# Output projection of a gated attention block: 16 parts of plain products replaced by one level of Strassen's scheme

## The chip, the cores and the metric

The kernel runs on one core of one Trainium2 chip. The metric is device time in microseconds (us), the median of several executions; the profile is of one execution. A core has five engines, each with one queue of instructions that it works through in order: PE (matrix products, results into the eight PSUM banks), DVE (vector work), ACT (activation functions and copies), POOL (GpSimd) and SP (here only a queue that issues transfers). POOL and ACT issue transfers too. Sixteen DMA engines carry all transfers.

## The reference, cut to what matters

```python
x  = L0_attn_x                                 # (2, 1024, 1024) f32
xn = _layernorm(x)
s  = attention(xn, wq, wk, wv) @ wo            # 32 heads of 32, 8 key heads, causal
g  = silu(ffn(xn, 4-bit weights, zeros, scales))   # 1024 -> 2 x 2752 -> 1024
return x + s * g
```

The change is in the last product of the attention, `out @ wo`: for each of the two batches a 1024 x 1024 matrix `wo` against 1024 tokens of 1024 channels, all in full float32. Its result waits in memory until the feed-forward block multiplies it in at the end.

## The kernel before

**Stages.** In this order: layer norm of batch 0; then for each batch the projections to queries, keys and values (`project`), the attention (`attend`), and the output projection (`project_out`); then the feed-forward block for both batches (`ffn_in_order`), which begins with the products `acc` of L1198. The weights of the feed-forward block come as 4-bit numbers. A generator, `unpack`, turns them into floats unit by unit beside the attention stages: its turns are called from the other stages as `next(side)`.

**The output projection.** `Output.oT` holds the attention's result, 128 partitions by 8 blocks (`NS`) of channels by 1024 tokens. Eight weight tiles `ws` (one for each 128 output channels, each with 8 blocks of 128 input channels) are loaded during the last two key heads. The work is cut into 16 `parts`: 256 tokens by two output blocks. A part is 16 products of 128x128 weights with 256 tokens (L880), eight into each half of one PSUM bank; then `leave` copies the bank to SBUF (L892, by DVE and ACT in turn) and stores it to `sT` (L893, from POOL's or ACT's queue). One float32 product is two matmul instructions in the trace, each with its own weight load.

**Inside the last head.** `first` makes two of the parts while the last key head is attended. It is a generator, and each `next(others)` in `attend` gives out one product of 256 tokens, to fill the time in which PE would wait for ACT's exponentials. The instructions of `attend` are in an order written by hand (`tc.manual_schedule`).

**Beside the other parts.** In `project_out` the order on each engine comes from a planner that lists instructions by program order and by its own estimate of when their inputs come; the queues then run in that order whatever comes late. Batch 0: at the end of each of the first eight parts one tile of batch 1's layer norm (`norm`, L326 to L342) is done: a load on SP's queue, statistics and scaling on DVE, eight transposes on PE, copies on ACT. From part seven on, `side` has `turns` = 3 turns twice in each part. Batch 1: no norm, and `side` has its turns from the first part on; the feed-forward block's inputs `x` and its first weights `w` are loaded at the same time from SP's queue (L946, L937).

**A unit of `unpack`** is four turns: SP loads `qw` and `zt` (L242, L244, two buffers each), DVE makes `nib` (L258, L260, L263), ACT writes `nf` (L267, two instructions of 128x1024), and POOL's queue stores `nf` (L249, 1 MB; two of 512 KB where it goes to `ng`). Batch 0's `project_out` does 8 units, batch 1's does 14. `nf` has the buffers that its pool is opened with: three here, two in the `project` of batch 1. What is left of `side` comes right after `project_out`. The feed-forward block lies in a conditional, so all its instructions stand behind all of `side` on every queue.

## Time and profile before

| | |
|---|---|
| median of 3 runs | 2293.79 us (2292.4 to 2294.47) |
| profiled execution, its own time | 2293.33 us |
| its span in the trace | 2291.6 us |
| granted TensorE clock, mean | 0.993 |
| output projection alone on PE, batch 0 (with 8 norm tiles) | 561.8 to 668 us |
| output projection alone on PE, batch 1 | 1191 to 1290 us |

Times within the trace are counted from the start of the span. A matmul's duration in a row covers its whole way through the array, and successive ones overlap, so the rate at which PE works is read from a stretch: instructions by time. An engine's idle time is put down to what ended it. A row of the timeline or of the chain gives start, length, engine, line and operation; brackets hold the idle time before it and its releaser. A row of windows gives each engine's busy time in a stretch, the granted clock, and the mean busy share of the DMA engines.

### The profile page before, as it was taken

How to read it: one execution, taken by the hardware profiler on the slowest of the kernel's cores; microseconds unless marked ns; L12 is line 12 of the kernel's file. 1: busy time of each engine (PE TensorE's matmuls, PEld its weight loads, DVE VectorE, ACT ScalarE, POOL GpSimd, SP SyncE). 2: the span in 40 equal slices, each digit the busy share in tenths (PEclk: the TensorE clock that was granted, in tenths of full speed). 3: DMA queues.
4: the chain of work that ended last, by engine and by line, in shares of the span. 5: the costliest groups of instructions: out<-in, count | busy, mean ns of one | idle time of the engine just before them, and what ended most of it. 6: DMA issues, size and time to landing. Idle time of an engine off the chain costs nothing.

```text
span 2291.6 us, 30825 instructions
## 1 busy us (share of the span) xinstructions
PE 2239.3 (98%) x11313; PEld 1537.5 (67%) x11313; DVE 1420.2 (62%) x2268; ACT 1132.3 (49%) x1819; POOL 792.4 (35%) x569
## 2 busy tenths in 40 slices
PE   7989999999999999999999999999999999999998
PEld 4455555555874465555558888888877888888875
DVE  5544677773324736777722367667877777777775
ACT  2102544553223325445533455555887555556875
POOL 1303677774035427776741100000234100001362
PEclk9999999999999999999999999999999999999999
DMA  5727323122468971231319623231846655323475
GB/s 180 220 91 244 80 47 93 38 75 76 129 210 280 301 215 47 52 88 38 80 54 344 181 56 83 55 83 55 303 138 219 176 137 139 96 71 105 137 231 154
DMA packets 262183, 309.50 MB, mean 135 GB/s; under 512 B 19147, under 2 KB 197707, under 8 KB 261880
## 3 DMA queue, kind: packets, MB, share of 16 engines
q1 hardware_dynamic: 245172, 260.62, 38.4%
q0 software_dynamic: 10752, 38.02, 5.2%
q10 hardware_dynamic: 6100, 8.82, 1.2%
q8 instruction: 91, 1.49, 0.3%
q14 instruction: 68, 0.56, 0.1%
HBM read 214.58 MB, written 97.03 MB: 136 GB/s over the span
## 4 chain that ended last, share of the span: by engine, by line
PE 82%; issue 7%; POOL 6%; DVE 2%; ACT 2%; DMA 1%; SPq 0%; ACTq 0%; POOLq 0%; DVEq 0%
PE acc L1198 27%; PE acc L1079 12%; PE ps_wo L880 10%; PE st L661 7%; PE s L554 7%; PE o L708 5%; PE ps_qk L384 5%; PE l L726 3%; PE st L676 2%; PE ps_v L407 1%; POOL rot L391 1%; PE s L548 1%; POOL rot L392 1%; POOL p L821 1%; ACT p L686 1%
## 5 line engine op out<-in xcount | busy, mean ns | idle before, releaser
L1198 PE MATMUL acc<-x,w 128*128 128x512 f32 x2752 | 640.1, 393 | 1.2 <-ACT gate L1169 0.9
L1198 PEld LDWEIGHTS acc<-x,w 128*128 128x128 f32 x2752 | 512.3, 188 | 120.5 <-DVE h L1171 7.2
L564 DVE TENSOR_REDUCE mx<-s 128x1 f32<-128x512 f32 (+3 forms) x672 | 384.8, 608 | 190.3 <-PE s L554 91.7
L968 DVE TENSOR_SCALAR acc<-acc,r_gu 128x1024 f32<-128x1024 f32 x301 | 389.1, 1293 | 166.5 <-PE acc L1198 164.9
L686 ACT ACTIVATE p<-st 128x512 f32<-128x512 f32 (+3 forms) x768 | 314.7, 497 | 316.8 <-PE st L676 314.6
L966 ACT ACTIVATE acc<-acc,r_gu 128x1024 f32<-128x1024 f32 x301 | 327.4, 1088 | 231.5 <-PE acc L1198 226.7
L1182 POOL TENSOR_TENSOR h_lo<-h,h_hi 128x512 fp32r<-128x512 f32 x78 | 100.3, 1287 | 805.2 <-DVE h L1160 300.6
L821 POOL TENSOR_TENSOR p<-p 128x2048 f32<-128x2048 f32 (+3 forms) x122 | 360.0, 2955 | 9.0 <-PE o L708 4.6
L968 DVE TENSOR_SCALAR acc<-acc,r_d 128x512 f32<-128x512 f32 x320 | 241.7, 759 | 62.0 <-PE acc L1079 59.3
L966 ACT ACTIVATE acc<-acc,r_d 128x512 f32<-128x512 f32 x320 | 210.8, 663 | 61.8 <-PE acc L1079 55.0
L384 PE MATMUL ps_qk<-xnT,w_qk 128*128 128x512 f32 x512 | 236.0, 602 | 2.5 <-DVE rot L390 2.5
L880 PE MATMUL ps_wo<-oT,w_o 128*128 128x256 f32 x1024 | 232.1, 382 | 0.0
L1079 PE MATMUL acc<-h_lo,w 128*128 128x512 f32 (+1 forms) x576 | 228.9, 397 | 3.0 <-POOL h_lo L1182 2.6
L1079 PE MATMUL acc<-h_hi,w 128*128 128x512 f32 (+1 forms) x576 | 229.5, 398 | 0.7 <-ACT h_hi L1181 0.7
L880 PEld LDWEIGHTS ps_wo<-oT,w_o 128*128 128x128 f32 x1024 | 191.1, 190 | 40.9 <-issue 16.7
L708 PE MATMUL o<-p,v 128*32 128x512 f32 (+3 forms) x1536 | 162.9, 496 | 0.9 <-POOL p L689 0.9
L384 PEld LDWEIGHTS ps_qk<-xnT,w_qk 128*128 128x128 f32 x512 | 94.6, 192 | 99.8 <-issue 93.4
L689 POOL TENSOR_SCALAR_AFFINE_SELECT p<-p 128x512 f32<-128x512 f32 x128 | 80.5, 636 | 163.5 <-ACT p L686 123.0
L391 POOL TENSOR_TENSOR rot<-rot,cs 128x512 f32<-128x512 f32 x40 | 51.3, 1283 | 239.6 <-DVE rot L390 230.2
L554 PE MATMUL s<-kst,room 128*128 128x512 f32 (+3 forms) x384 | 130.4, 379 | 0.0
L1079 PEld LDWEIGHTS acc<-h_lo,w 128*128 128x128 f32 (+1 forms) x576 | 108.4, 188 | 31.0 <-POOL h_lo L1182 5.4
L1079 PEld LDWEIGHTS acc<-h_hi,w 128*128 128x128 f32 (+1 forms) x576 | 108.3, 188 | 30.6 <-issue 2.9
(163 smaller groups left out, 2405.7 us busy)
## 6 DMA issues: line engine op xcount, KB each, us to landing
w<-ng SPq DMA_DIRECT2D x86, 512.0 KB, 5.2
w<-nd SPq DMA_DIRECT2D x63, 512.0 KB, 4.0
ng<-nf POOLq DMA_DIRECT2D x42, 512.0 KB, 6.9
room<-qs SPq DMA_DIRECT2D x160, 128.0 KB, 4.0
x<-xs SPq DMA_DIRECT2D x32, 512.0 KB, 10.2
qst<-qs SPq DMA_DIRECT2D x96, 128.0 KB, 3.8
xt<-in_L_attn_x SPq DMA_DIRECT2D x16, 512.0 KB, 6.2
w_qk<-in_L_attn_wq SPq DMA_DIRECT2D x16, 512.0 KB, 5.0
```

Of the source, the lines that this page charges most:

```text
L384: nc.tensor.matmul(ps, w[:, s, :], xnT[:, s, tok], start=(s == 0), stop=(s == NS - 1))
L554: nc.tensor.matmul(s[:, c * w : (c + 1) * w], q[j][:, qt * P : (qt + 1) * P], k[:, k0:k1], start=n == 1, stop=c == n - 1 and (n > 1 or not ...
L564: nc.vector.tensor_reduce(mx[:, at, js[0] : js[0] + n, k0 // TB], s[:, : w * n].rearrange("p (j t) -> p j t", j=n), AX.X, ALU.max)
L661: nc.tensor.matmul(s[:, q0:], kst[g][:, kt * P : (kt + 1) * P], stack[g][j][:, qlo + q0 : qlo + TB], start=True, stop=False,)
L686: nc.scalar.activation(p[:, j, q0:], st[j][:, q0:], AF.Exp, scale=1.0 / math.sqrt(HD))
L708: nc.tensor.matmul(o[HD * j : HD * (j + 1), q0:], v[:, kt, HD * g : HD * (g + 1)], p[:, j, q0:], start=(kt == 0), stop=last,)
L821: what(*args)
L880: self.last = nc.tensor.matmul(ps[:, c * self.BLK : (c + 1) * self.BLK], self.ws[c0 + c][:, g, :], self.oT[:, g, t0 : t0 + self.BLK], star ...
L966: nc.scalar.mul(a, a, r)
L968: nc.vector.tensor_scalar(a, a, r, None, ALU.mult)
L1079: nc.tensor.matmul(acc[c], w[:k, c * P : (c + 1) * P], ht[:k, :], start=(f == 0 and t == 0), stop=(t == 1), skip_group_check=(f > 0),)
L1198: nc.tensor.matmul(a[:, n, :], w[i][:, g * P : (g + 1) * P], xs[t][:, g, n * TB : (n + 1) * TB], start=(g == 0 and t == 0), stop=(t == 1), ...
```

## The change

The projection of each pair `i` of output blocks (four pairs) becomes one level of Strassen's scheme in Winograd's form. The halves are: output block `c` of the pair, input half `k` (four blocks of 128 channels, `H` = 4), token half `n` (512 tokens). `A[n, k]` are the quarters of `oT`, `weights(i, k, c)` those of the weights. Seven products take the place of eight; each is four matmuls of 128x128 with 512 tokens.

- Sums of the tokens are made once for a batch, by DVE, in 128x2048 pieces: `s1` in a new tile, and three in the places of `A[1, 0]`, `A[0, 0]` and `A[0, 1]` once these have been used.
- Sums of the weights are made for each pair (`quarters`): two by DVE (one into `t_2`), two by POOL, each 128x512.
- Products one and two of every pair come first. Those of pairs 0 and 1 are `first`, inside the last head, with two `yield`s for each product of 512 tokens; DVE copies both. Those of pairs 2 and 3 open `rest`; ACT copies them.
- Then five products for each pair, in two banks `a` and `b`. Each bank is read between its two products: `b` by DVE (`u2`), `a` by ACT (`p5`, to which POOL adds `p1`). Product `fourth` goes into `b` a third time, after the next pair's first product. Four results leave for each pair; of the 16 stores of a batch, 14 are issued by POOL and 2 by ACT, where it was 8 and 8.
- `rest` yields 24 times in a batch, once after each product. `project_out` gives `side` its 3 turns at each (in batch 0 from the eighth on), and the norm's tiles come one after each of the first eight.
- The pool `wo_out` has two buffers for a name instead of four, one for `p_5`, `s_1` and `t_2`. The `unpack` pool of these stages has two buffers instead of three: two for `nf`.

```diff
--- before.py
+++ after.py
@@ -799,7 +799,7 @@
                     output.load(0, NREP + 1)
                 if qb == 0 and kt == 0 and g == NKV - 1:
                     output.load(NREP + 1, NC)
-                    others = output.first(head.ps)
+                    others = output.first(head.ps, kp)
                 if qb == 0 and kt == 0 and 0 < g < NKV - 3:
                     kst.append(key_stack(g + 3))
                 if kt == 0:
@@ -858,12 +858,20 @@
     class Output:
-        BLK = 256
+        H = NS // 2
+        PAIRS = NC // 2
         def __init__(self, b, oT, pool):
             self.b, self.oT, self.pool = b, oT, pool
             self.ws = []
-            self.parts = [(t0, c) for t0 in range(0, T, self.BLK) for c in range(0, NC, 2)]
+            H = self.H
+            self.A = {
+                (n, k): oT[:, k * H : (k + 1) * H, n * TB : (n + 1) * TB] for n in range(2) for k in range(2)
+            }
+            self.p1, self.banks = {}, {}
         def load(self, c0, c1):
             for c in range(c0, c1):
@@ -872,41 +880,122 @@
                 self.ws.append(w)
                 nc.sync.dma_start(w, wo[:, c * P : (c + 1) * P].rearrange("(g p) n -> p g n", p=P))
-        def products(self, part, ps):
-            t0, c0 = part
-            for c in range(2):
-                for g in range(NS):
-                    self.last = nc.tensor.matmul(
-                        ps[:, c * self.BLK : (c + 1) * self.BLK],
-                        self.ws[c0 + c][:, g, :],
-                        self.oT[:, g, t0 : t0 + self.BLK],
-                        start=(g == 0),
-                        stop=(g == NS - 1),
-                    )
-                    yield g
-        def leave(self, part, ps, r):
-            t0, c0 = part
-            copy, queue = ((nc.vector.tensor_copy, nc.gpsimd), (nc.scalar.copy, nc.scalar))[c0 // 2 % 2]
-            copy(r, ps)
-            queue.dma_start(
-                sT_dram[self.b][:, c0 : c0 + 2, t0 : t0 + self.BLK], r.rearrange("p (c t) -> p c t", c=2)
-            )
-        def first(self, pools):
-            r = self.pool.tile([P, 2 * TB], F32, name="wo_r", tag=f"room_{NREP}")
+        def weights(self, i, k, c):
+            return self.ws[2 * i + c][:, k * self.H : (k + 1) * self.H]
+        def product(self, ps, w, x, first):
+            for s in range(self.H):
+                self.last = nc.tensor.matmul(
+                    ps, w[:, s, :], x[:, s, :], start=first and s == 0, stop=s == self.H - 1, skip_group_check=not first
+                )
+                yield
+        def leave(self, i, c, n, y, queue):
+            queue.dma_start(sT_dram[self.b][:, 2 * i + c, n * TB : (n + 1) * TB], y)
+        def first(self, pools, kp):
+            keep = self.pool.tile([P, 2, TB], F32, name="p_1", tag=f"room_{NREP}")
+            r = kp.tile([P, 2, TB], F32, name="wo_r", tag="kst_1")
             for i in range(2):
-                ps = pools[i].tile([P, TB], F32, name="ps_wo", tag=f"s_{i}")
-                part = self.parts.pop(0)
-                yield from self.products(part, ps)
-                self.leave(part, ps, r[:, i * TB : (i + 1) * TB])
+                ps = self.banks[i] = pools[i].tile([P, TB], F32, name="ps_wo", tag=f"s_{i}")
+                for _ in self.product(ps, self.weights(i, 0, 0), self.A[0, 0], True):
+                    yield
+                    yield
+                self.p1[i] = keep[:, i]
+                nc.vector.tensor_copy(self.p1[i], ps)
+            for i in range(2):
+                ps = self.banks.pop(i)
+                for _ in self.product(ps, self.weights(i, 1, 0), self.A[0, 1], False):
+                    yield
+                    yield
+                nc.vector.tensor_copy(r[:, i], ps)
+                self.leave(i, 0, 0, r[:, i], nc.gpsimd)
+        def rest(self, pool, psp):
+            A, weights = self.A, self.weights
+            def bank():
+                return psp.tile([P, TB], F32, name="ps_wo")
+            def product(*args):
+                for _ in self.product(*args):
+                    pass
+            def tile(name, **kw):
+                return pool.tile([P, TB], F32, name=name, **kw)
+            s1 = pool.tile([P, self.H, TB], F32, name="s_1", bufs=1)
+            nc.vector.tensor_tensor(s1, A[1, 0], A[1, 1], ALU.add)
+            nc.vector.tensor_tensor(A[1, 0], A[0, 0], A[1, 0], ALU.subtract)
+            more = range(2, self.PAIRS)
+            for i in more:
+                self.banks[i] = bank()
+                product(self.banks[i], weights(i, 0, 0), A[0, 0], True)
+                self.p1[i] = tile("p_1")
+                nc.scalar.copy(self.p1[i], self.banks[i])
+                yield
+            nc.vector.tensor_tensor(A[0, 0], s1, A[0, 0], ALU.subtract)
+            t2 = {}
+            def quarters(i):
+                t2[i] = pool.tile([P, self.H, P], F32, name="t_2", bufs=1)
+                nc.vector.tensor_tensor(weights(i, 0, 0), weights(i, 0, 1), weights(i, 0, 0), ALU.subtract)
+                nc.vector.tensor_tensor(t2[i], weights(i, 1, 1), weights(i, 0, 0), ALU.subtract)
+                nc.gpsimd.tensor_tensor(weights(i, 0, 1), weights(i, 1, 1), weights(i, 0, 1), ALU.subtract)
+                nc.gpsimd.tensor_tensor(weights(i, 1, 0), weights(i, 1, 0), t2[i], ALU.subtract)
+            quarters(0)
+            for i in more:
+                product(self.banks[i], weights(i, 1, 0), A[0, 1], False)
+                r = tile("u_2")
+                nc.scalar.copy(r, self.banks.pop(i))
+                self.leave(i, 0, 0, r, nc.scalar)
+                yield
+            nc.vector.tensor_tensor(A[0, 1], A[0, 1], A[0, 0], ALU.subtract)
+            def fourth(i, b):
+                product(b, weights(i, 1, 0), A[1, 1], False)
+                nc.vector.tensor_tensor(self.p1[i], b, self.p1[i], ALU.add)
+                self.leave(i, 0, 1, self.p1[i], nc.gpsimd)
+            ahead = None
+            for i in range(self.PAIRS):
+                b = bank()
+                product(b, t2[i], A[0, 0], True)
+                u2 = tile("u_2")
+                nc.vector.tensor_tensor(u2, b, self.p1[i], ALU.add)
+                yield
+                if ahead:
+                    fourth(*ahead)
+                    yield
+                a = bank()
+                product(a, weights(i, 0, 0), s1, True)
+                p5 = tile("p_5", bufs=1)
+                nc.scalar.copy(p5, a)
+                nc.gpsimd.tensor_tensor(p5, p5, self.p1[i], ALU.add)
+                if i + 1 < self.PAIRS:
+                    quarters(i + 1)
+                yield
+                product(b, weights(i, 0, 1), A[1, 0], False)
+                nc.vector.tensor_tensor(p5, b, p5, ALU.add)
+                self.leave(i, 1, 1, p5, nc.gpsimd)
+                yield
+                product(a, weights(i, 1, 1), A[0, 1], False)
+                nc.vector.tensor_tensor(u2, a, u2, ALU.add)
+                self.leave(i, 1, 0, u2, nc.gpsimd)
+                yield
+                ahead = i, b
+            fourth(*ahead)
+            yield
     def project_out(output, side, turns, xnT, xp):
         with ExitStack() as st:
-            res = st.enter_context(tc.tile_pool(name="wo_out", bufs=4, reuse_waits="tile"))
+            res = st.enter_context(tc.tile_pool(name="wo_out", bufs=2, reuse_waits="tile"))
             psp = st.enter_context(tc.tile_pool(name="wo_ps", bufs=6, space=PSUM, reuse_waits="tile"))
             following = iter(())
             w_k = None
@@ -916,20 +1005,17 @@
                 following = norm(output.b + 1, xnT, ln, ln_ps, 3)
                 w_k = load_kv(xp, wk)
             normed = None
-            for i, part in enumerate(output.parts):
-                ps = psp.tile([P, TB], F32, name="ps_wo")
-                for g in output.products(part, ps):
-                    if g == 0 and (xnT is None or i >= NT - 1):
-                        with ExitStack() as order:
-                            for last in normed or ():
-                                order.enter_context(tc.issue_after(last.ins))
-                            for _ in range(turns):
-                                next(side, None)
+            for i, _ in enumerate(output.rest(res, psp)):
+                if xnT is None or i >= NT - 1:
+                    with ExitStack() as order:
+                        for last in normed or ():
+                            order.enter_context(tc.issue_after(last.ins))
+                        for _ in range(turns):
+                            next(side, None)
                 with tc.issue_after(output.last.ins):
                     normed = next(following, normed)
-                output.leave(part, ps, res.tile([P, TB], F32, name="wo_r"))
             return w_k
     def load_gu(ring, f, u):
@@ -1480,7 +1566,7 @@
             xnT = xp = None
         else:
             x_open, xnT, xp = open_x()
-        with tc.tile_pool(name="unpack", bufs=3, side="right", reuse_waits="tile") as up:
+        with tc.tile_pool(name="unpack", bufs=2, side="right", reuse_waits="tile") as up:
             side = unpack(up, range(8) if b == 0 else range(20, NF), b == B - 1)
             w_k = project_out(output, side, 3, xnT, xp)
             for _ in side:
```

## The prediction

> **What bounds the kernel now.** I read the page first (busy shares, chain, costliest groups), then the chain in order of time, the busy time by stretches, and in the two projection stages each engine's timeline and waits.
>
> ```profile
> span 2291.6 us, 30825 instructions
> ...
> PE 2239.3 (98%) x11313; PEld 1537.5 (67%) x11313; DVE 1420.2 (62%) x2268; ACT 1132.3 (49%) x1819; POOL 792.4 (35%) x569
> ...
> L880 PE MATMUL ps_wo<-oT,w_o 128*128 128x256 f32 x1024 | 232.1, 382 | 0.0
> ```
>
> PE is the bound, and the changed line L880 is 232 us of it, 116 a batch, with no idle time before it. The chain shows the rates:
>
> ```profile
> 626.50 41.44 PE ps_wo L880 x192
> 667.94 56.65 PE ps_qk L384 x132
> ...
> 1191.03 99.06 PE ps_wo L880 x458
> ```
>
> An instruction of 256 columns takes 41.44/192 = 0.2158 us, one of 512 columns 56.65/132 = 0.4292 us (L384, same type and weights). So wider matmuls alone win nothing; only fewer products do. The stretches (columns: PE, PEld, DVE, ACT, POOL busy, clock, DMA share, GB/s) show what else is full:
>
> ```profile
> 561.80:668.00 106.20, 106.20 (x527) 93.94 (x524) 34.33 (x83) 31.32 (x49) 20.07 (x26) 1.00 0.67 208
> 1191.00:1290.00 99.00, 99.00 (x463) 87.17 (x460) 23.83 (x67) 30.84 (x35) 18.89 (x23) 1.00 0.93 309
> ```
>
> PE has no gap in either, at a granted clock of 1.00. DVE, ACT and POOL are a third busy or less. But in batch 1 the DMA engines are 93% busy, and the queues that carry the unpacking wait for them (ACT's timeline, then waits, batch 1):
>
> ```profile
> 1249.46 2.00 ACT L267 ACTIVATE nf<-nib 128x1024 fp32r<-128x1024 uint8 x2 [2.32 <-DMA nd<-nf]
> 1253.14 2.00 ACT L267 ACTIVATE nf<-nib 128x1024 fp32r<-128x1024 uint8 x2 [1.68 <-DMA nd<-nf]
> 1257.53 2.00 ACT L267 ACTIVATE nf<-nib 128x1024 fp32r<-128x1024 uint8 x2 [2.38 <-DMA nd<-nf]
> 1259.44 0.56 ACT L892 COPY wo_r<-ps_wo 128x512 f32<-128x512 f32 x1
> ...
> 1277.35 2.00 ACT L267 ACTIVATE nf<-nib 88x1024 fp32r<-88x1024 uint8 x2 [4.97 <-DMA nd<-nf]
> 1279.25 0.56 ACT L892 COPY wo_r<-ps_wo 128x512 f32<-128x512 f32 x1
> ```
> ```profile
> DVE nib L263 <- DMA zt<-zb_d: 17.1, 6, 5.0
> ACT nf L267 <- DMA nd<-nf: 16.8, 7, 5.0
> ```
>
> The copies of finished banks stand in these queues. The tenth part of the stage ended on PE at about 1193 + 10 x 6.9 = 1262; ACT copied it at 1279.25, 17 us late. That cost nothing before: six banks of 6.9 us each are 41 us of room.
>
> **The change part by part.**
>
> *Products.* Per batch, 256 matmuls of 256 columns become 112 of 512; in instructions, 512 x 0.2158 = 110.5 us become 224 x 0.4292 = 96.1 us. `first` keeps its share (32 of 256, then 16 of 112: 13.8 us both), so `rest` falls from 448 x 0.2158 = 96.7 us to 192 x 0.4292 = 82.4 us: 14.3 us a batch, 28.6 in all. A product of `rest` is 3.43 us.
>
> *`first`, inside the last head.* Same work in pieces of 0.86 us at every other turn instead of 0.43 at each. PE was busy 40.8 of 42 us there (520 to 562). Between +1 and -1 us: I take 0. The DVE copies (0.69 us, L892) come when DVE is idle (9.13 us before the last `lt`), and the bank has the other pair's product (3.4 us) before it is written again.
>
> *Token sums.* Four DVE operations of 128x2048. The 128x512 sum of L753 takes 0.68 us undisturbed; four times the elements about 2.3. The last `oT` comes at 1193.6 (batch 1), so `s1` ends at 1196, `A[1,0]` at 1198, `A[0,0]` after products one (1200) at 1202.5; two `quarters` (0.68 each) follow to 1204. PE wants `t_2` at 1193 + 4 x 3.43 = 1207. Hidden, by 3 us. In batch 0, DVE also has norm tiles: 2.4 us each (two statistics 0.65, L329, and L337 0.83, small ones), and PE wants one every 3.43 + 0.88 = 4.3 us instead of every 7.8. Divide, three sums, quarters and five tiles are 2.1 + 6.9 + 1.4 + 12 = 22 us; by the fifth product PE has given 19 to 20. PE waits 2 us (0 if the first loads come before the divide; 5 if sums and late `xt` loads line up).
>
> *Weight sums and `p5`.* Per batch 8 DVE operations (5.4 us), and on POOL 8 plus 4 for `p5` at 1.28 us (L753 on POOL), 15.4 us; the bank sums are 16 reads of 0.7 us, half of them where copies were. DVE goes to about 34 + 9.2 + 5.4 + 5.6 = 54 of 92 us in batch 0, 44 of 85 in batch 1, POOL to 35: room. That two engines' sums collide has a row:
>
> ```profile
> 1161.82 4.57 POOL L821 TENSOR_TENSOR p<-p 128x2048 f32<-128x2048 f32 x1 [2.31 <-PE o L708]
> ...
> 1162.78 4.15 DVE L753 TENSOR_TENSOR oT<-oc,rt 128x512 f32<-128x512 f32 x1
> ```
>
> The DVE sum, 0.68 us elsewhere, lasted until POOL's ended. New POOL operations are 1.28 us, so a collision costs at most that: at most 15.4 us of DVE time a batch, hidden by DVE's idle third. I take 0; the bound is 3 us, the four sums ahead of PE's first need. [...]
>
> *Banks.* This is what the change adds to the path. `a` may be written again only after ACT's `p5`, with one product between (3.43 us of room; before, 41). `p5` stands in ACT's queue among the `nf` that wait for DMA; `u2` and the other sum in DVE's queue among the `nib`; POOL's share of `p5` among the stores. What is late by more than 3.43 us stops PE. Also `p_5` has one buffer: its next copy waits for the store of the last, four products later (13.7 us against 0.7 + 0.75 + 8.7 for sum, issue and landing in batch 1): hidden while POOL isn't 3 us late.
>
> *`nf` with two buffers.* A buffer's cycle in batch 1 is 2.0 (ACT) + 0.3 + 0.86 (POOL's issue) + 8.8 us to landing = 12.0; by three, 4.0 us a unit (the rows above: 3.7 and 4.4). By two, with the landing unchanged, 6.0; with the shortest landing of L249, 3.5 us, 3.3, so nothing lost. The DMA engines were 0.9 to 1.0 busy, so much of the 8.8 is queueing behind the third buffer and falls with it: I take 4.4, nearer the low end.
>
> *Batch 0.* PE alone would end at 668 - 14.3 = 653.7. Unpacking now begins after the seventh norm tile at about 595 (619 before) and takes 8 x 4.6 us (before 34 us) plus waits, to 632 to 635. The `p5` at products 11 and 16 (609 and 626) lie inside; the late ACT copy of 644.17 shows 4 us of lag with three buffers. One stop of 3 us: with DVE's 2, PE loses 5. Gain 14.3 - 5 = 9 (3 to 14).
>
> *Batch 1.* The unpacking is held by 8 MB of `x` and by `w` until 1230 (`qw`, 15.4 us wait), then 13 units, four of 88 rows and a small one. They took 48 us, 12 x 4.0; 12 x 4.4 put the last `nf` at 1284 to 1286 instead of 1279. PE alone would end at 1275.7. But `p5` of the last pair stands near the last `nf`; two products (6.9 us) follow it: 1286 + 0.6 + 6.9 is beyond the old end, 1290, by some 3 us if it stands behind all of them, and before it, 1285, if two units remain. I take a gain of 0.5 (bounds -20 with 6.0 us a unit: 12 x 2 us later; +12 if the lag never reaches PE, since the feed-forward block's ACT work still stands behind the last `nf` at 1279).
>
> *Queues.* SP keeps its loads in number and order. POOL issues 14 instead of 8 stores a batch (0.74 us each): inside its idle 80%.
>
> Sum: 9 + 0.5 = 9.5 us off the profiled execution's 2293.33 (span 2291.6 and 1.7 around it): 2283.8; its median stands 0.46 higher: 2284.
>
> **The rivals.**
>
> *Both stages pay in full.* For it: PE had no gap, engines are two thirds idle, and the planner may set `p5` ahead of `nf`. Against: the 17 us lag. Gain 13 + 11 = 24: 2270.
>
> *Batch 1 gives back what batch 0 brings.* Lag and unpacking hold each other up: ACT waits for PE's `a` while `nf` waits behind it. Some 5 us a unit: last `nf` at 1291, PE's end at 1299, 9 - 9 = 0: 2294.
>
> *Slower: two `nf` buffers hold the stage.* With the landing at 8.8 us a unit takes 6.0; batch 1's last `nf` is at 1303, PE's end at 1310 (-20); batch 0's 8 units end at 643, with PE's stops 10 us (+4). Together -16: 2310. It decides from 5.3 us a unit on: last `nf` at 1294, PE's end at 1302 (-12), batch 0 at +7, so -5, just over 0.2%. Against it: DMA share near 1.0 means that the landing is queueing.
>
> *The saving isn't one*, because 512-column matmuls are slower than two of 256: excluded by 0.4292 against 2 x 0.2158.
>
> **How the numbers follow.** Forecast 0.40 (2278 to 2289), both in full 0.23 (2266 to 2277), given back 0.16 (2289 to 2299), slower 0.21 (2299 to 2312). 0.2%, 4.6 us, is about what a measurement can tell here from no change. Faster 0.63, same 0.16, slower 0.21. The range leaves out the slow half of the last case and the best of the second: 2267 to 2303.
>
> **What would show it.** Right: L880's place holds 2 x 224 instructions of 512 columns at 0.43 us; PE gaps before second and third products into a bank, ended by ACT `p_5` or DVE sums, behind `nf` and `nib` waiting for DMA; batch 1's first `acc` within 5 us of 1290 less batch 0's gain. Wrong: no gaps there (2270), or units at 5.3 us and more (over 2298), or PE waiting in batch 0 for norm transposes by more than 5 us.

## The result, and the profile after

The changed kernel takes 2302.9 us (median of 5 runs, 2300.53 to 2305.48); the kernel before, in the same comparison, 2293.79 (2292.4 to 2296.23). The ratio is 1.0037 with a 95% interval of 1.0026 to 1.0048: slower by 9 us or 0.4%. The forecast was 2284, faster by 0.4%.

Three lines of the page of the changed kernel. L889 is now the projection's matmul, L1284 the feed-forward block's.

```profile
span 2300.8 us, 29810 instructions
...
PE 2216.2 (96%) x10737; PEld 1427.9 (62%) x10737; DVE 1483.4 (64%) x2316; ACT 1132.8 (49%) x1819; POOL 837.2 (36%) x605
...
L889 PE MATMUL ps_wo<-oT,w_o 128*128 128x512 f32 x320 | 153.5, 619 | 20.8 <-ACT p L978 14.4
```

PE does 23 us less (2239.3 before) in a span that is 9.2 us longer. The saving was made, and something else grew by more. The last line says where: before L889 PE is idle for 20.8 us, mostly released by ACT's copy of `p5` (L978). Before the change that column read 0.0.

The two projection stages, as stretches (columns as before: length, then PE, PEld, DVE, ACT and POOL busy, clock, DMA share, GB/s):

```profile
562.80:663.00 100.20, 92.49 (x264) 43.45 (x261) 57.60 (x102) 31.88 (x49) 36.51 (x38) 1.00 0.65 207
1188.60:1299.00 110.40, 90.74 (x198) 38.56 (x196) 50.77 (x87) 31.53 (x36) 39.31 (x38) 0.94 0.85 284
```

Batch 0's stage went from 106.2 to 100.2 us. Batch 1's went from 99.0 to 110.4: its PE work is shorter, but there is a hole of 20 us in it, and the mean granted clock is 0.94 where it was 1.00. The whole difference, cut at the same events in both traces (start of the second-last single mask of batch 0's last head, last sum matmul `l` of L726 in each batch, first `ps_qk` of L384, first `acc` of the feed-forward block, end):

| stretch | before, us | after, us | difference |
|---|---|---|---|
| up to the mask in batch 0's last head | 539.86 | 539.44 | -0.4 |
| from it to the last `l` | 21.60 | 22.98 | +1.4 |
| projection, batch 0 | 106.32 | 100.59 | -5.7 |
| projections and attention of batch 1, up to the same mask | 501.23 | 502.19 | +1.0 |
| from it to the last `l` | 21.60 | 22.99 | +1.4 |
| projection, batch 1 | 99.12 | 110.87 | +11.8 |
| feed-forward block | 1001.87 | 1001.74 | -0.1 |
| span | 2291.6 | 2300.8 | +9.2 |

Two things need an explanation: the projection of batch 1, and 1.4 us in each last head. First the projection, on PE's timeline of the changed kernel (start, length, what, idle time before and its releaser):

```profile
1209.07 3.60 PE L889 MATMUL ps_wo<-s,w_o 128*128 128x512 f32 x8
...
1254.75 5.40 PE L889 MATMUL ps_wo<-oT,w_o 128*128 128x512 f32 x8 [4.32 <-ACT p L978]
...
1268.47 7.13 PE L889 MATMUL ps_wo<-oT,w_o 128*128 128x512 f32 x16 [1.45 <-DVE p L984]
1282.38 5.43 PE L889 MATMUL ps_wo<-oT,w_o 128*128 128x512 f32 x8 [6.79 <-ACT p L978]
1292.77 5.36 PE L889 MATMUL ps_wo<-oT,w_o 128*128 128x512 f32 x8 [4.96 <-DVE p L984]
1299.06 6.20 PE L1284 MATMUL acc<-x,w 128*128 128x512 f32 x26 [0.94 <-PE ps_wo L889]
```

A product takes 3.43 us start to start, as forecast. Each of the four stops shown before L889 is at a second or third product into a bank. They sum, with one of 1.27 us at 1205.53 and the 0.94 at the end, to 19.7 us. And the product after each of the three long stops takes 5.4 us instead of 3.6: another 5.4 us. What ACT did at the longest stop:

```profile
1279.86 2.00 ACT L267 ACTIVATE nf<-nib 88x1024 fp32r<-88x1024 uint8 x2 [4.72 <-DMA nd<-nf]
1281.77 0.56 ACT L978 COPY p<-ps_wo 128x512 f32<-128x512 f32 x1
1287.47 2.00 ACT L267 ACTIVATE nf<-nib 88x1024 fp32r<-88x1024 uint8 x2 [5.14 <-DMA nd<-nf]
```

The product into the bank (`ps_wo<-s,w_o` at 1263.42, 3.60 us) ended at 1267.0. Its copy comes 15 us later: it stands in ACT's queue behind an `nf` that waits 4.72 us for a store to land. Then POOL's half of `p5`, on POOL's timeline:

```profile
1289.79 0.91 POOL L249 DMA_DIRECT2D nd<-nf  x1 [6.15 <-ACT nf L267]
1290.63 1.36 POOL L979 TENSOR_TENSOR p<-p,p 128x512 f32<-128x512 f32 x1
```

Here `p5` stands behind the issue of the last unit's store, which waits 6.15 us for the last `nf`, which waits 5.14 us for DMA. DVE's sum (L984, 1292.02) waits for POOL, and PE for DVE. So `p5` of the last pair is held twice, once in each queue that it goes through. The waits of 1226 to 1300 us sum it up (us, times, longest):

```profile
ACT nf L267 <- DMA nd<-nf: 25.8, 9, 5.1
...
PE ps_wo L889 <- ACT p L978: 11.1, 2, 6.8
...
PE ps_wo L889 <- DVE p L984: 6.4, 2, 5.0
```

The lengthened products are a matter of the clock. Windows of the changed kernel, one over an unbroken stretch and one from the end of each long stop:

```profile
1205.50:1246.00 40.50, 40.47 (x95) 17.99 (x96) 21.25 (x37) 10.22 (x12) 17.01 (x16) 1.00 0.88 294
1254.75:1260.00 5.25, 5.25 (x9) 2.23 (x10) 1.79 (x7) 2.00 (x2) 2.02 (x3) 0.67 0.99 356
1282.40:1287.60 5.20, 5.20 (x8) 2.07 (x8) 0.00 (x0) 0.13 (x1) 1.24 (x2) 0.66 0.84 249
1292.80:1298.00 5.20, 5.20 (x8) 2.05 (x8) 0.00 (x0) 0.00 (x0) 0.55 (x1) 0.68 0.64 192
```

After stops of 4.3, 6.8 and 5.0 us the granted clock is about two thirds for the next 5 us.

Second, the last head. POOL's timeline of the changed kernel in batch 0, and PE's at the same time:

```profile
547.86 1.26 POOL L948 TENSOR_TENSOR w_o<-w_o 128x512 f32<-128x512 f32 x1 [0.63 <-DVE w_o L946]
549.08 1.23 POOL L689 TENSOR_SCALAR_AFFINE_SELECT p<-p 128x512 f32<-128x512 f32 x2
```
```profile
549.77 0.64 PE L708 MATMUL o<-p,v 128*32 128x256 f32 x8 [1.35 <-POOL p L689]
```

Before, the masks of L689 started at 547.96 and PE did not wait. The planner has put the first weight sum of pair 0, which the program makes in `rest`, into POOL's queue ahead of the last two masks of attention.

### The profile page after: what moved, and what is told of

It reads as the page before. It is cut to its first block, busy times and chain, and to the rows that moved or that the text cites. A ratio compares the mean times of both kernels' runs of the same rounds, so it can differ in the third digit from the quotient of the medians.

```text
span 2300.8 us, 29810 instructions
## 1 busy us (share of the span) xinstructions
PE 2216.2 (96%) x10737; PEld 1427.9 (62%) x10737; DVE 1483.4 (64%) x2316; ACT 1132.8 (49%) x1819; POOL 837.2 (36%) x605
## 4 chain that ended last, share of the span: by engine, by line
PE 60%; POOL 3%; DMA 3%; issue 3%; DVE 2%; ACT 2%; SPq 1%; POOLq 0%; DVEq 0%; ACTq 0%
PE acc L1284 27%; PE acc L1165 12%; PE ps_qk L384 4%; PE st L661 3%; PE s L554 3%; PE ps_wo L889 3%; PE o L708 3%; PE l L726 1%; PE ps_v L407 1%; PE st L676 1%; DMA nd<-nf 1%; DMA ng<-nf 1%; POOL p L821 1%; POOL y L1205 1%; ACT nf L267 1%
## 5 line engine op out<-in xcount | busy, mean ns | idle before, releaser
L1284 PE MATMUL acc<-x,w 128*128 128x512 f32 x2752 | 639.0, 393 | 1.9 <-PE ps_wo L889 0.9
L1284 PEld LDWEIGHTS acc<-x,w 128*128 128x128 f32 x2752 | 512.4, 188 | 120.8 <-DVE h L1257 7.2
L384 PE MATMUL ps_qk<-xnT,w_qk 128*128 128x512 f32 x512 | 236.1, 602 | 2.5 <-DVE rot L390 2.5
L889 PE MATMUL ps_wo<-oT,w_o 128*128 128x512 f32 x320 | 153.5, 619 | 20.8 <-ACT p L978 14.4
L384 PEld LDWEIGHTS ps_qk<-xnT,w_qk 128*128 128x128 f32 x512 | 94.6, 192 | 99.9 <-issue 93.5
L689 POOL TENSOR_SCALAR_AFFINE_SELECT p<-p 128x512 f32<-128x512 f32 x128 | 81.0, 640 | 161.7 <-ACT p L686 121.3
L394 ACT CAST rot_hi<-rot 128x512 fp32r<-128x512 f32 x40 | 24.6, 618 | 204.6 <-POOL rot L392 181.0
```

Source lines behind the costliest of these rows:

```text
L384: nc.tensor.matmul(ps, w[:, s, :], xnT[:, s, tok], start=(s == 0), stop=(s == NS - 1))
L889: self.last = nc.tensor.matmul(ps, w[:, s, :], x[:, s, :], start=first and s == 0, stop=s == self.H - 1, skip_group_check=not first)
L1284: nc.tensor.matmul(a[:, n, :], w[i][:, g * P : (g + 1) * P], xs[t][:, g, n * TB : (n + 1) * TB], start=(g == 0 and t == 0), stop=(t == 1), ...
```

## The experiments

Theories. **Queues:** the projection of batch 1 is longer because `p5` stands in queues (ACT's, then POOL's) behind unpacking that waits for its stores. **Two buffers:** it is longer because `nf` has two buffers instead of three. **The products:** the scheme's seven products save nothing near 14 us in this place. For the last head: **the weight sum** on POOL, against **the granularity** of `first` (pieces of 512 tokens instead of 256).

**Two buffers alone, in the kernel before.**

```diff
-        with tc.tile_pool(name="unpack", bufs=3, side="right", reuse_waits="tile") as up:
+        with tc.tile_pool(name="unpack", bufs=2, side="right", reuse_waits="tile") as up:
             side = unpack(up, range(8) if b == 0 else range(20, NF), b == B - 1)
```

> The kernel before, with nothing changed but two buffers instead of three for nf beside the output projection. Theory A (each bank has one product of room, 3.4 us, so PE stops when ACT's p5 stands in its queue behind nf that waits for its store): here six banks of 6.9 us give room, so PE has no gap; the last nf of batch 1 moves from 1279 to about 1289 us, PE still ends at 1290, the time is 0 to +4 us. Theory B (the two buffers alone cost it, with any scheme): +8 us or more, with PE idle before or right after the first acc.

Measured: 2294.08 us, ratio 1.0001 (0.9992 to 1.001). PE has no stop in the projection. The transfers' median time from issue to landing, for the 1 MB stores of `nf`, first before, then with two buffers:

```profile
nd<-nf POOLq DMA_DIRECT2D x8, 1024.0 KB, 8.8
```
```profile
nd<-nf POOLq DMA_DIRECT2D x8, 1024.0 KB, 6.2
```

With one store fewer under way the median landing is 2.6 us sooner. The last `nf` starts 95.5 us after the last `l` instead of 86.7, and is still in time for a projection of 99 us. The third buffer cost nothing to give up there, and the two-buffer theory falls as a cause by itself. The changed kernel with a third buffer and nothing else was not run, so what two buffers add to the stops behind `p5` stays open.

**The products with nothing beside them.** Batch 1's unpacking is put wholly behind the projection.

```diff
-                if xnT is None or i >= NT - 1:
+                if xnT is not None and i >= NT - 1:
...
-            for _ in side:
-                pass
+            with ExitStack() as behind:
+                if xnT is None:
+                    behind.enter_context(tc.issue_after(output.acts.ins))
+                    behind.enter_context(tc.issue_after(output.sums.ins))
+                for _ in side:
+                    pass
```

> The changed kernel, with all of batch 1's unpacking put behind the last p5 and the last sum of the output projection, on ACT and DVE. Theory A: batch 1's projection on PE runs without stops after the first (1.3 us): 88 us from the end of the attention, ending near 1275 us instead of 1298, at a clock of 1.00; the unpacking then lies bare, some 55 us, and the whole is slower, 2320 to 2335. Theory C (the sums on DVE and POOL are too slow for PE, whatever stands beside them): PE keeps stops of 15 us and more.

Measured: 2338.34 us in one run. PE's timeline (the feed-forward block, which waits for its weights), and the window of the projection:

```profile
1273.93 3.00 PE L1284 MATMUL acc<-x,w 128*128 128x512 f32 x12 [0.96 <-PE ps_wo L889]
1333.06 7.11 PE L1284 MATMUL acc<-x,w 128*128 128x512 f32 x23 [56.12 <-ACT acc L1052]
```
```profile
1188.00:1272.80 84.80, 83.43 (x195) 36.59 (x193) 27.49 (x29) 4.68 (x8) 25.08 (x22) 1.00 0.46 166
```

From the last `l` to the first `acc` it is 87.3 us, of which 1.37 are a stop at its start and 0.96 the one at its end: 85.0 at clock 1.00, where the forecast had 84.8 for PE alone (99.1 less 14.3). So the products save what they should, and the theory that they don't falls. The 56 us wait shows what the unpacking is worth beside them.

**`p5` without ACT and POOL.** One DVE operation reads the bank and adds `p1`.

```diff
-                nc.scalar.copy(p5, a)
-                nc.gpsimd.tensor_tensor(p5, p5, self.p1[i], ALU.add)
+                nc.vector.tensor_tensor(p5, a, self.p1[i], ALU.add)
```

> The changed kernel, with p5 made by one DVE operation from the bank and p1, instead of ACT's copy and POOL's addition. Theory A: PE's waits for ACT p5 (3.3, 4.3, 6.8 us) and for the sum behind POOL (5.0 us) go; DVE's queue has waits too (nib behind nf), so some 3 to 8 us come back there. Time 2288 to 2298. Theory B: PE's end in batch 1 stays tied to the last nf, 1298: within 3 us of the changed kernel. Theory C: more on DVE, so the same or slower.

Measured: 2285.26 us (2283.26 to 2287.41), ratio 0.9963 (0.995 to 0.9976). This one edit turns 9 us of loss into 8.5 us of gain. Stops are left in the projection of batch 1 (PE's timeline; one more of 1.54 us at its start):

```profile
1248.13 3.70 PE L889 MATMUL ps_wo<-oT,w_o 128*128 128x512 f32 x8 [1.04 <-DVE p L978]
...
1269.33 9.88 PE L889 MATMUL ps_wo<-oT,w_o 128*128 128x512 f32 x16 [3.77 <-DVE p L978]
1280.14 3.01 PE L1283 MATMUL acc<-x,w 128*128 128x512 f32 x12 [0.94 <-PE ps_wo L889]
1284.22 5.98 PE L1283 MATMUL acc<-x,w 128*128 128x512 f32 x25 [1.07 <-ACT acc L1051]
```

The projection of batch 1 is 95.6 us, that of batch 0 96.3. The queue theory holds. DVE's queue holds `p5` too, behind `nib` that waits for ACT's `nf`, but less long. The last line is the next bound: the feed-forward block's first ACT work stands behind the last `nf`.

**More room instead of a shorter way.** `p5` stays with ACT and POOL; two pairs are interleaved, so that between the first two products into a bank there are three others or more, where `a` had one.

```diff
+            for what, i in (
+                (b1, 0), (a1, 0), (b1, 1), (a1, 1), (b2, 0), (a2, 0), (b1, 2), (a1, 2), (d, 0), (b2, 1),
+                (a2, 1), (b1, 3), (a1, 3), (d, 1), (b2, 2), (a2, 2), (b2, 3), (d, 2), (a2, 3), (d, 3),
+            ):
+                what(i)
+                yield
...
+                p5[i] = weights(i, 0, 0).rearrange("p g n -> p (g n)")
...
-                r = tile("u_2")
+                r = tile("u_2", bufs=3)
```

Here `b1` and `b2` are the first and second product into bank `b`, `a1` and `a2` those into `a`, `d` the `fourth`.

> The changed kernel, with the same products in another order: two pairs are under way at once, so that 3 to 7 products lie between the two uses of a bank instead of 1 or 2 (p5 takes the place of the first weight quarter, which is used up by then; u_2 has three buffers). Two nf buffers as in the changed kernel. Theory A: the stops on p5 and the sums shrink to 0 to 6 us in both batches; PE's end in batch 1 is then set by the last nf (1289) only through the feed-forward block's ACT work: 2285 to 2294. Theory B: no gain, 2300 to 2305, since the unpacking is as slow as it was.

Measured: 2288.91 us (2286.1 to 2290.93), ratio 0.9977 (0.9968 to 0.9987). PE's timeline:

```profile
1262.00 10.57 PE L889 MATMUL ps_wo<-oT,w_o 128*128 128x512 f32 x24 [1.98 <-DVE w_o L984]
1274.94 4.47 PE L1291 MATMUL acc<-x,w 128*128 128x512 f32 x12 [2.38 <-issue]
1284.40 21.35 PE L1291 MATMUL acc<-x,w 128*128 128x512 f32 x84 [4.99 <-ACT acc L1059]
```

Two stops, 1.31 and 1.98 us, are all that is left in the projection, with the same operations in the same queues: the lateness is harmless given room. But PE reaches the feed-forward block 6.4 us before the last `nf` starts (1281.38) and then waits for it, and the block starts at a granted clock of 0.65 (over the 5.6 us from 1284.40 on): the 84 instructions after the wait take 21.35 us.

**`first` in pieces of 256 tokens.** As written here, the sum of products one and two of pairs 0 and 1 is not complete, neither in this kernel nor in the two further down that contain it. In the program the second half of product one opens its sum in a bank in which the first half still waits for product two; no run shows whether that is the cause. Instructions, sizes and waits are those of the whole computation, so these kernels are used for their times alone.

```diff
+                for n in range(2):
+                    cols = slice(n * TB // 2, (n + 1) * TB // 2)
+                    for g in range(self.H):
+                        self.last = nc.tensor.matmul(
+                            ps[:, cols],
+                            w[:, g, :],
+                            x[:, g, cols],
...
-                for _ in self.product(ps, self.weights(i, 0, 0), self.A[0, 0], True):
-                    yield
-                    yield
+                yield from halves(ps, self.weights(i, 0, 0), self.A[0, 0], True)
```

> The changed kernel, with the four products inside the last head made in pieces of 256 tokens again, one for each turn, as before the change. Theory: the attention of each batch lost 1.8 us because a filler of 512 tokens at every other turn leaves PE waiting at the turn between (1.35 us on POOL's p) and pushes the rest back; in pieces of 256 it comes back: last l 1.5 to 1.8 us earlier in each batch, and 2298 to 2301 us in all, since what follows moves along. Rival (the loss comes from the DVE copies or from the order by hand): no change, 2301 to 2305.

Measured: 2305.55 us, ratio 1.0049 (1.0033 to 1.0066). PE's timeline in the last head:

```profile
550.17 0.64 PE L708 MATMUL o<-p,v 128*32 128x256 f32 x8 [1.71 <-POOL p L689]
```

The wait for the mask is there as in the changed kernel (1.71 us instead of 1.35). The granularity is not it.

**The 88-row units mixed in.** The last four large units of batch 1 have 88 rows instead of 128, and in the changed kernel they follow one another at 4.8, 6.7 and 7.6 us where the others take 4.0 to 4.6. This kernel, on top of `p5` by DVE, takes them in turn with the units of 128 rows.

```diff
-            for r0 in range(0, RD if down else 0, P):
-                r1 = min(RD, r0 + P)
-                for c0 in range(0, D, 2 * P):
+            for c0 in range(0, D if down else 0, 2 * P):
+                for r0 in range(0, RD, P):
+                    r1 = min(RD, r0 + P)
```

> The kernel of e3 (p5 by one DVE operation), with batch 1's units of unpacking in another order: each unit of 88 rows follows two of 128 rows, where the four of 88 rows stood at the end. Theory: the stores of 88 rows land 12 us after issue against 6.5 us for 128 rows, and with two nf buffers they cannot overlap enough at the end (7.6 us between the last units); mixed, the last nf ends 2 to 5 us earlier than e3's 1283, and the feed-forward block starts as much earlier: 2280 to 2284. Rival (the DMA engines' total work sets it): last nf within 1.5 us of e3's, same time.

Measured: 2293.22 us, ratio 0.9998 (0.9988 to 1.0008): 8 us slower than without the edit. PE's stop in the last pair grew from 3.77 to 8.23 us, again behind DVE's `p5`, and the last `nf` starts at 1286.54 instead of 1281.19. That the tail is slow because its units come last is wrong. ACT's timeline shows what is slow:

```profile
1282.47 2.01 ACT L267 ACTIVATE nf<-nib 128x1024 fp32r<-128x1024 uint8 x2 [6.91 <-DMA nd<-nf]
```

With two buffers, the unit that starts at 1282.47 takes over the buffer of an 88-row unit. The three units that do so start 6.6, 7.7 and 8.9 us after the one before them, the others after 1239 us 3.4 to 4.6. With `p5` by DVE alone the stores of 88 rows (704 KB) land at a median of 8.3 us, those of 128 rows (1 MB) at 5.9. With the four at the end, only two of their buffers are taken over; mixed, three are.

**Three edits together.** Interleaved pairs, `p5` by DVE, halves in `first`; also `wo_r` in another place, because DVE's first `t_2` waited 4.7 us for the store of `wo_r`, whose place it takes over.

```diff
-            r = kp.tile([P, 2, TB], F32, name="wo_r", tag="kst_1")
+            r = kp.tile([P, 2, TB], F32, name="wo_r", tag="kst_2")
...
-                nc.scalar.copy(p5[i], a[i])
-                nc.gpsimd.tensor_tensor(p5[i], p5[i], self.p1[i], ALU.add)
+                nc.vector.tensor_tensor(p5[i], a[i], self.p1[i], ALU.add)
```

> The changed kernel with four edits: pairs interleaved as in e4, p5 by one DVE operation as in e3, the first products in pieces of 256 tokens as in e5, and the result of first in another used-up place (kst_2 instead of kst_1), which t_2 doesn't overlap. Two nf buffers. Theory: PE's stops in the projection go nearly altogether (under 3 us a batch, and the first DVE sums no longer wait for the store of first's result); batch 1's feed-forward block then starts when the last nf is done, some 1280: 2278 to 2284. If it is within 1 us of e3, the last nf alone sets the end.

Measured: 2287.48 us, ratio 0.9972 (0.9962 to 0.9981), not better than `p5` by DVE alone. The projection is nearly free of stops, and that is the trouble (PE's timeline, then a window from the restart):

```profile
1274.43 3.00 PE L1300 MATMUL acc<-x,w 128*128 128x512 f32 x12 [3.37 <-issue]
1284.15 22.22 PE L1300 MATMUL acc<-x,w 128*128 128x512 f32 x84 [6.72 <-ACT acc L1068]
```
```profile
1284.10:1290.00 5.90, 5.85 (x14) 4.61 (x15) 1.54 (x2) 2.08 (x2) 2.83 (x5) 0.50 0.77 209
```

The last `nf` (1281.13) sets the end, as in the kernel with `p5` by DVE (1281.19). PE stands idle for 6.72 us before it, in one piece, and pays for it with half the clock: the 84 instructions after the wait take 22.2 us here and 19.50 there. Being early cost 2.7 us.

**The third buffer back.** The same, with three `nf` buffers. Room for the third is made by keeping `s_1` in two places of the feed-forward block's weight ring.

```diff
+        places = [xp.tile([P, 2, TB], F32, name=f"s_1{j}", tag=f"w_{4 + j}") for j in range(2)]
...
-        with tc.tile_pool(name="unpack", bufs=2, side="right", reuse_waits="tile") as up:
+        with tc.tile_pool(name="unpack", bufs=3, side="right", reuse_waits="tile") as up:
```

> The kernel of e7 with three nf buffers: room for the third is made by putting s_1, in batch 1, into two of the feed-forward block's six weight buffers, which are loaded only after the projection. Theory: the last nf of batch 1 comes some 7 us earlier, at 1272 to 1276, and PE's own work (82.4 us) is then the bound: 2270 to 2277. Rival (buffers don't matter since the DMA engines are full): within 2 us of e7.

Measured: 2282.68 us (2279.72 to 2283.9), ratio 0.9949 (0.9932 to 0.9966). The last `nf` starts 87.0 us after the last `l` (96.4 with two buffers, in the run above), and the feed-forward block no longer waits for it. A stop of 3.09 us behind DVE remains. So two buffers cost nothing in the old scheme, and some 5 us (2287.48 less 2282.68) as soon as the projection is short enough.

**The weight sum kept out of attention.** One ordering edge on POOL, in the changed kernel.

```diff
-                    nc.gpsimd.affine_select(
+                    output.mask = nc.gpsimd.affine_select(
...
-                nc.gpsimd.tensor_tensor(weights(i, 0, 1), weights(i, 1, 1), weights(i, 0, 1), ALU.subtract)
+                with tc.issue_after(self.mask.ins):
+                    nc.gpsimd.tensor_tensor(weights(i, 0, 1), weights(i, 1, 1), weights(i, 0, 1), ALU.subtract)
```

> The changed kernel with one edge more on POOL's queue: the first weight sum of each pair (w(i,0,1), 1.26 us) may not be issued ahead of the last causal mask of the attention. In the changed kernel pair 0's sum stood in the last head ahead of the last two masks, and attention ended 1.8 us later in each batch. Theory that this sum is what attention lost: PE's wait on a mask in the last head (1.35 us before, 1.71 with the change cut in halves) falls back to what it was with the old kernel, the last sum matmul of attention in batch 0 comes at about 561 us instead of 562.4, and the time falls by 2 to 3.6 us to about 2300. Rival that the first products themselves cost attention the 1.8 us: attention ends where it did, the time stays at 2303. The batch 1 projection is expected unchanged in either case (stops of 4 to 7 us behind p_5 and the clock falling after them).

Measured: 2304.74 us (2301.37 to 2305.53), ratio 1.0048 (1.0034 to 1.0061): no faster. Yet the last head is as long as it was before the change: 21.57 us from the mask to the last `l` in both batches, against 22.98 and 22.99, and PE does not wait for a mask. The sum is the cause of the longer head, as the theory says, but the kernel gains nothing that the measurement shows. In batch 1 the projection took the time back: 112.2 us instead of 110.9. Where the 1.4 us of batch 0 went is not shown: the profiled execution is the fastest of the five, and its span of 2299.3 us is 1.5 us below that of the changed kernel. The stops behind `p5` are the same (4.22, 6.94 and 4.53 us), and the clock after them fell further:

```profile
1252.40:1257.60 5.20, 5.16 (x6) 2.19 (x7) 1.88 (x7) 2.00 (x2) 2.06 (x3) 0.50 0.97 352
1280.30:1285.50 5.20, 5.20 (x6) 2.19 (x7) 0.00 (x0) 0.00 (x0) 1.26 (x2) 0.50 0.89 236
```

Over the third, from 1291.10 us, it is 0.55. The product after each stop takes 6.56, 6.28 and 6.00 us instead of 5.40, 5.43 and 5.36.

**The same edge, and `p5` by DVE.** The edge above, and again:

```diff
-                nc.scalar.copy(p5, a)
-                nc.gpsimd.tensor_tensor(p5, p5, self.p1[i], ALU.add)
+                nc.vector.tensor_tensor(p5, a, self.p1[i], ALU.add)
```

> The same edge on POOL's queue, and the fifth term's sum p_5 made by one DVE operation straight from the bank instead of an ACT copy and a POOL sum (as in the earlier run with 2285.3 us). If the two losses (p_5 behind the dequantisation on ACT and POOL; the weight sum inside attention) are separate, the gains add: 2285.3 less 2 to 3.6 us is 2282 to 2283. If the end is set by the last dequantised unit, which started 1281.2 us in that run, and it moves with attention, the same; if that unit does not move because the stores behind it set it, the gain of batch 1 is lost in a wait for acc of the FFN and the time is 2283.5 to 2285.

Measured: 2286.0 us (2283.44 to 2288.56), ratio 0.9964 (0.995 to 0.9978): the same as without the edge. The last case of the expectation came out, 1 us above its range. PE reaches the feed-forward block 2.2 us earlier (1277.93 instead of 1280.14) and waits there 2.77 us for the last `nf` instead of 1.07 (1280.66 instead of 1281.19), with a granted clock of 0.68 in the 5.3 us after it where it was 1.00.

**All of it.** Interleaved pairs, `p5` by DVE, three buffers, `wo_r` in the other place, the edge on POOL, `first` as in the changed kernel, and the load of `w_kv` in batch 0 written behind four of the norm's loads. New against the diffs above:

```diff
-                w_k = load_kv(xp, wk)
...
                     normed = next(following, normed)
+                if xnT is not None and i == 3:
+                    w_k = load_kv(xp, wk)
```

> All that the runs point to together: two pairs interleaved, p_5 by one DVE operation in a place used up, the third buffer for dequantised rows (s_1 in two places of the FFN's weight ring), wo_r in the other key place, the weight sum behind the last mask, and in batch 0 the key weights' load behind the first four token tiles' loads. The run with all but the last two gave 2282.7, with a PE stop of 2.73 us in batch 0 where DVE had waited 4.72 us for a token tile. Expected: both attentions 1.8 us earlier and that stop gone, 2276 to 2280. Rival (the dequantised rows set the end whatever the projection does): their last unit stays at 1275 and the FFN's start at 1279, and the time at 2281 to 2283.

Measured: 2275.28 us (2273.67 to 2277.63), ratio 0.9922 (0.9908 to 0.9935): 18.4 us better than the kernel before, just below what was expected, and better than every other kernel here. PE's timeline of batch 1 and the window of its stage:

```profile
1258.86 10.54 PE L889 MATMUL ps_wo<-oT,w_o 128*128 128x512 f32 x24 [1.76 <-DVE w_o L990]
1270.23 22.20 PE L1298 MATMUL acc<-x,w 128*128 128x512 f32 x96 [0.83 <-issue]
```
```profile
1183.10:1270.20 87.10, 84.54 (x196) 36.99 (x196) 46.97 (x92) 28.34 (x32) 25.46 (x29) 1.00 0.95 320
```

The stage takes 87.6 us from the last `l` to the first `acc`, where it was 99.1 before and 110.9 after the change, at clock 1.00 and with the DMA engines 95% busy. The last `nf` starts at 1269.23, with the end of the projection. The rival of the expectation, that this unit would stay where it was, falls: it comes 86.6 us after the last `l`, so it moves with attention. The edit of `w_kv` did not do its part: the planner issued that load first all the same (564.39 us, the norm's at 571.01), and the stop of batch 0 stayed (3.02 us behind DVE's `rstd`, after a DVE wait of 4.56 us for a token tile). Batch 0's stage is 98.4 us, 2 us more than with `p5` by DVE alone.

## Why the prediction was wrong

**Right: the products.** 3.43 us a product, and `rest` 14.3 us shorter with nothing beside it (85.0 us for the stage). The rival that the saving isn't one fell.

**Right: the place and the cause.** The forecast named the step that lets ACT's queue onto the path: one product of room for a bank, `p5` behind `nf`, stops at the second and third product into a bank. All are in the trace.

**Half right: two buffers.** The forecast had 4.4 us a unit, with landing times that fall because less is under way. In batch 1 the units of 128 rows took 4.0 to 4.6, and alone in the old kernel it cost nothing. The rival with 6.0 us a unit fell. But the last `nf` came 99.3 us after the last `l`, 12.5 us later than before (86.7) instead of 5 to 7. Two buffers alone, in the old scheme, make it 8.8 us later (95.5). With `p5` by DVE it comes at 96.6, so 2.7 us of the 12.5 go with `p5` in the queues of ACT and POOL. The four units of 88 rows add 2.5: from the first to the last it is 19.1 us, and 16.6 before.

**Wrong: "SP keeps its loads in number and order".** The loads for batch 1's first unit, before and after the change (SP's timeline):

```profile
1140.08 1.99 SPq L242 DMA_DIRECT2D qw<-in_L_ffn_qweight_gu  x2
```
```profile
1216.37 2.17 SPq L242 DMA_DIRECT2D qw<-in_L_ffn_qweight_gu  x2
```

They stood ahead of the loads of `x` and `w` and now stand behind them. The first `nf` of the stage starts at 1226.19 instead of 1194.63, so all 14 units come after those loads, where the forecast counted 13. In batch 0 the first three token tiles of the norm are loaded from 566.54 us on instead of 558.98. No run put the old order back, so what this costs is not shown.

**Batch 0: gain 9 forecast, 5.7 measured.** It is inside the bounds of 3 to 14. The `p5` stop was forecast as 3 us and is 3.32. The stops on DVE's side were forecast as 2 and are 4.4 (1.86, 0.41, 0.52, 0.61, 0.98).

**Wrong: batch 1, a gain of 0.5 forecast, a loss of 11.8 measured.** This is the step that failed, by 12 us, and it alone turns the sign. It was inside the step's bounds (-20 to +12), but for other reasons than the lower bound's. Three terms were missing from the sum or far too small in it:

- In batch 1 `p5` was priced once, as the last copy behind the last `nf`, "3 us if it stands behind all of them". It stopped PE at pairs 2 and 3, and the second half of `p5` was held again in POOL's queue behind the store of the last `nf`. The forecast did name POOL's queue and gave it no price. Four stops together are 17.5 us (4.32, 1.45, 6.79, 4.96); `p5` by one DVE operation left 4.8 of them.
- The clock after a stop: 5.4 us for three restarts. The forecast had no such term; no row of the two stages before the change had a stop in it.
- DVE's `t_2` behind the store of `wo_r`, whose place it takes over: in batch 1 DVE waited 4.7 us and PE 1.3, and in the last kernel above, with `wo_r` elsewhere, this stop is gone. The forecast listed the token sums one by one and held them "hidden, by 3 us", without asking whose memory `t_2` takes. In batch 0 DVE has the same wait (4.5 us), but there it is not the cause of PE's 1.86 us: with `wo_r` elsewhere (three edits together) DVE waits 4.5 us for a token tile instead, and PE still 1.48, against 1.47 with the pieces of 256 tokens alone.

**Wrong: `first`, 0 with bounds of 1 us; 1.4 us in each last head.** The size of the pieces was harmless, as argued. What failed was to price only `first` for the last head: the planner may move any operation of `rest` into it whose inputs are ready, and a 1.26 us sum ahead of a mask costs 1.4 us on PE. With the edge the head is short again and the kernel no faster, so how much of the 9 us these heads are stays open. Another 1.0 us in the stretch ahead of batch 1's last head is no more than that stretch varies by: over all the runs here it is 500.95 to 502.19 us.

**The collisions of DVE and POOL** were taken as 0, with a bound of 3 us. They came: in batch 1 POOL's sum L949 took 3.19 us instead of 1.28, and DVE's L946 1.76 instead of 0.68. The bound had priced DVE waiting for a POOL sum of 1.28 us, not POOL waiting for a DVE sum of 2.29. That POOL sum started 0.2 us after a DVE sum of 2.29 and ended 1.1 us after it. Both lie ahead of the 1.3 us stop. What they cost PE by themselves is not shown; the kernel with three edits makes the same sums on the same two engines, and PE has no stop at that place.

**The rivals.** "Batch 1 gives back what batch 0 brings" (2294) had the mechanism closest to what happened, lag in ACT's queue and PE holding each other up, but without POOL and the clock it stopped at no change. The slower rival, two buffers, gave 2310 for a wrong reason.

## What to carry to other kernels

When a change takes away the slack between two uses of a buffer, price every operation between them with the wait of what stands ahead of it on each queue that it passes. A result that goes through two queues can pay twice, as it did here, and the row to price it with is the lag that was free before (17 us here). Do such a step in one operation on the queue that waits least, or put more independent work between the two uses. And when one end gets earlier, look for what it meets next: here the last `nf`, which two buffers alone made 8.8 us later at no cost, until the projection was shorter. Check also that the planner left the loads where they were.

## What the runs showed of the hardware that was not expected

After some of PE's stops the granted clock was lower, and the length of the stop alone did not decide it. In the two projection stages and at the start of the feed-forward block it was, in windows of 3.6 to 7 us at the restart:

| stop of PE, us | granted clock after it |
|---|---|
| 4.22, 4.32, 4.53, 4.96, 4.99, 6.72, 6.79, 6.94, 8.23 | 0.50 to 0.69 |
| 2.38, 2.77, 3.02, 3.09, 3.63, 3.77 | 0.50 to 0.69 |
| 2.73, 3.32, 3.37, 3.45, 3.71 | 1.00 |
| 0.98, 1.04, 1.07, 1.12, 1.27, 1.45, 1.86 | 1.00 |

Where a stop was followed by 8 matmuls that take 3.6 us elsewhere, they took 3.7 us after stops of 2.66, 3.32, 3.45 and 3.71 us, and 5.1 to 6.6 us after one of 3.46 and nine of 4.22 to 7.21.

Of the four stops under 3.1 us with a lower clock after them, those of 2.38 and 2.77 us lie at the start of the feed-forward block, close to other waits. Before 3.02 and 3.09 PE had worked for 13.9 us and more without a stop.

So in these runs PE's idle time cost less in small pieces than in one: the kernel with three edits reached the feed-forward block 5.7 us earlier than the one with `p5` by DVE alone (1274.43 against 1280.14), waited 6.72 us there in one stop, and took 2.2 us longer.
